# First half prepared by chunk, and the last batch's rows written whole, in a selective-scan and routed-attention kernel

## The chip, the cores and the metric

The kernel runs on one core of a Trainium2 chip, in float32. The metric is the device time of one execution in microseconds (us), a median over runs. On the core, TensorE (PE; PEld is its weight load), VectorE (DVE), ScalarE (ACT) and GpSimd (POOL) compute, each with an instruction queue of its own that it works through in order; SyncE (SP) and the queues of ACT and POOL issue transfers (DMAs), which sixteen DMA engines carry out. SBUF and PSUM are the memories on the core.

## The reference

Inputs are `x`, 16 batches of 1024 tokens and 512 channels, and weights. Two layers follow one another, both with a residual:

```python
# layer 1: selective scan over the tokens, 16 states a channel
xn = layernorm(x)
xp = xn @ x_proj_w.T                  # 64 + 16 + 16 columns: rank, B, C
delta = softplus(xp[..., :64] @ dt_proj_w.T + dt_proj_b)
h = exp(delta * A) * h + delta * B * xn        # A = -exp(A_log), token after token
x1 = x + sum_over_states(h * C) + xn * D

# layer 2: the 127 tokens of a batch with the highest router weight, and no others,
# go through attention and a feed-forward net
y = layernorm(x1)
w = y @ router_w + router_b
sel = the 127 tokens of largest w, in the order of tokens
x2 = block(y[sel])                    # attention with RoPE and mask, GELU net, residuals
out = x1 + where(selected, w * x2, y)
```

(`block`'s RMS norms, mask and heads play no part in the change. One more token, the one at the threshold, counts as not selected.)

## The kernel before

**Layer 1** (`scan_layer`) handles a batch in two halves of 512 tokens; there are 32 halves. A half has 16 states times 4 chunks of 128 channels, 64 steps (`per_half`), one hardware scan (`recur`, L329) of 128 channels by 512 tokens each. The order of all work is written out by hand (`tc.manual_schedule()`): a loop over the steps issues, for each, the diagonal matrices from memory (`diagonals`, L283), scaled rows (`scaled`, L296), decays (`decays`, L304), matmuls that bring the input products into place (`turn`, L316 and L318), the scan, and what follows it. Beside this loop run generators that are advanced once a step; `until(k)` lets one wait for step `k` of the half.

What a half needs beforehand is made by two of these generators, under the half before it. `stats(b)` takes mean and variance of 8 tiles of 128 tokens (`bn_stats` and `bn_aggr`, L138 and L139, on DVE) and makes `rstd` and `off` of them (Ln L142, Exp L144 on ACT, L146 on DVE). `prep(b, half)` normalises 4 tiles (L160, ACT), transposes them (L169, PE; L171, ACT), projects (L176, L180), stores the C rows and the diagonals of B to memory (L183, L187), and computes softplus per chunk of 128 channels (L208 to L218) up to a sum `rest` and an argument `delta`. At step `LN_AT` = 40 one Ln runs over all of `delta` (L230, 128 by 2048), POOL adds `rest` in two instructions (L233), PE transposes the result (L243), and DVE multiplies it with the normalised tokens to `du` (L247).

The first half has no half before it. There, ahead of the loop, the kernel issues `load(0)` (two DMAs of 1 MB, L119, on SP's queue), all of `stats(0)`, `cleared(0)`, a DMA that fills a 2 MB field in memory with zeros (L109, ACT's queue), and all of `prep` for the first half, each drained to its end. `cleared(1)` fills the second field. Only then the loop starts. The zero tile that `cleared` reads shares four buffers with the diagonals `dg`. The constants (`xp_sb` L70, `dt_sb` L74 and L75, `a_sb` L79 with its Exp on ACT L80 and the sign on DVE L81, `d_row` L83, from it `d_ps` L85 and `d_col` L87, `eye` L92, `skip` L95) stand ahead of the hand-written part, and a scheduler places them; they use the same queues.

**Layer 2** (`ffn_layer`) runs the 16 batches as a pipeline of stages (`scores`, `select`, `keep_others` and `attention`, `feed`), 28 steps a period. `select` computes each token's rank and gathers the selected rows of `x1` (`x1_sel`, printed as `x_sel`, L730) and of the mask (L726) with indirect DMAs. `keep_others` writes every row of `out` (L797): `x1 + y` for a token that isn't selected, `x1` for one that is. `feed`, the last stage, adds the net's result to `xs` (L944), multiplies by the router weight (L945), and adds the 127 rows to `out` with an indirect DMA that accumulates in memory (L946, issued by POOL). After the last batch's one the program ends.

Of the kernel before, what the change touches and what calls it, by code (L numbers as in the profile page):

```python
# [10 lines left out]
F32 = mybir.dt.float32  # L11
I32 = mybir.dt.int32
U32 = mybir.dt.uint32
AF = mybir.ActivationFunctionType
ALU = mybir.AluOpType
# [4 lines left out]
P = 128  # L20
# [7 lines left out]
def _drain(gen):  # L28
    for _ in gen:
        pass  # L30
# [3 lines left out]
def scan_layer(ctx, tc, x, x1_dram, a_log, dskip, xpT, dtT, dtb, ident):  # L34
# [9 lines left out]
    nc = tc.nc  # L44
    B, L, D = x.shape
    N = a_log.shape[1]
    R, E = dtT.shape[0], xpT.shape[1]
    ND = D // P
    NT = L // P
    LH = 512  # L50
    NH = L // LH
    TH = LH // P
# [10 lines left out]
    pool = ctx.enter_context(tc.tile_pool(name="s_pool", bufs=2))  # L63
# [2 lines left out]
    psy = ctx.enter_context(tc.tile_pool(name="s_psy", bufs=1, space=PSUM))  # L66
    psm = ctx.enter_context(tc.tile_pool(name="s_psm", bufs=4, space=PSUM))

    xp_sb = const.tile([P, ND, E], F32, tag="xp_sb", name="xp_sb")
    nc.sync.dma_start(xp_sb, xpT.rearrange("(c p) e -> p c e", p=P))  # L70

# [39 lines left out]
            zero.rearrange("p c q -> p (c q)").unsqueeze(1).to_broadcast([P, N, TD * P]),  # L111
        )

    xt, norm, ready, carry, rows_c = {}, {}, {}, {}, {}

    def load(b):
        xt[b] = pool.tile([P, NT, D], F32, tag="xt", bufs=1, name=f"xt_{b}")
        for q in range(NH):
            nc.sync.dma_start(  # L119
                xt[b][:, q * TH : (q + 1) * TH, :],  # L120
                x[b, q * LH : (q + 1) * LH, :].rearrange("(c p) d -> p c d", p=P),
            )

    clock = [0]

    def until(k):
        while clock[0] < k:
            yield

    def stats(b):  # L130

        st = small.tile([P, NT, nc.vector.BN_STATS_DIM], F32, tag="st", name=f"st_{b}")
        mv = small.tile([P, NT, nc.vector.BN_AGGR_DIM], F32, tag="mv", name=f"mv_{b}")
        rstd = small.tile([P, NT], F32, tag="rstd", name=f"rstd_{b}")
        off = small.tile([P, NT], F32, tag="off", name=f"off_{b}")
        for c in range(NT):
            yield from until(25 + 7 * c // 4)
            nc.vector.bn_stats(st[:, c, :], xt[b][:, c, :])  # L138
            nc.vector.bn_aggr(mv[:, c, :], st[:, c, :])  # L139

        yield from until(LN_AT)
        nc.scalar.activation(rstd, mv[:, :, 1], AF.Ln, bias=eps)  # L142
        yield from until(LN_AT + 1)
        nc.scalar.activation(rstd, rstd, AF.Exp, scale=-0.5)  # L144
        yield from until(LN_AT + 3)
        nc.vector.scalar_tensor_tensor(off, mv[:, :, 0], -1.0, rstd, ALU.mult, ALU.mult)  # L146
        norm[b] = (rstd, off)

    def bank(name):
        return psm.tile([P, 512], F32, tag="m", name=name)  # L150
# [1 line left out]
    def prep(b, half):  # L152

        s = f"{b}_{half}"
        rstd, off = norm[b]
        u = pool.tile([P, TH, D], F32, tag="u", bufs=1, name=f"u_{s}")
        for c in range(TH):
            yield from until(1 + c)
            q = half * TH + c
            nc.scalar.activation(  # L160
                u[:, c, :], xt[b][:, q, :], AF.Identity,
                bias=off[:, q : q + 1], scale=rstd[:, q : q + 1],
            )
        uT = pool.tile([P, ND, LH], F32, tag="uT", name=f"uT_{s}")
        for c in range(TH):
            yield from until(10 + 2 * c)
            tp = bank(f"tpu_{s}_{c}").rearrange("p (c f) -> p c f", c=ND)
            for dc in range(ND):
                nc.tensor.transpose(tp[:, dc, :], u[:, c, dc * P : (dc + 1) * P], ident)  # L169
            yield from until(11 + 2 * c)  # L170
            nc.scalar.copy(uT[:, :, c * P : (c + 1) * P], tp)  # L171
        yield from until(19)
        pp = bank(f"pp_{s}")
        for dc in range(ND):
            yield from until(19 + dc // 2)
            nc.tensor.matmul(  # L176
                pp[:E, :], xp_sb[:, dc, :], uT[:, dc, :], start=(dc == 0), stop=(dc == ND - 1)
            )
        yield from until(21)
        nc.scalar.copy(xp[:E, :], pp[:E, :])  # L180
        yield from until(22)
        bc = dram.tile([N, LH], F32, tag="bc", name=f"bc_{s}")
        nc.sync.dma_start(bc, xp[R + N : E, :])  # L183
        h = halves.index((b, half))
        rows_c[h] = bc
        for c in range(TD):
            nc.sync.dma_start(  # L187
                fields[h % 2].rearrange("n (p r) -> n p r", r=TD * P + 1)[:, :, c * P],
                xp[R : R + N, c * P : (c + 1) * P],
            )  # L190
        tb = bank(f"tb_{s}")[:, : TH * 2 * N].rearrange("p (c e) -> p c e", c=TH)
        for c in range(TH):
            nc.tensor.transpose(
                tb[:, c, :], xp[R:E, c * P : (c + 1) * P], ident[R:E, R:E]
            )
        yield from until(23)
        bT = small.tile([P, TH, N], F32, tag="bT", name=f"bT_{s}")
        nc.scalar.copy(bT, tb[:, :, :N])


        delta = pool.tile([P, ND, LH], F32, tag="delta", name=f"delta_{s}")
        rest = pool.tile([P, ND, LH], F32, tag="rest", bufs=1, name=f"rest_{s}")

        def softplus(dc, k):
            yield from until(k)
            z = bank(f"z_{s}_{dc}")
            e, t = delta[:, dc, :], rest[:, dc, :]
            nc.tensor.matmul(z, dt_sb[:, dc * P : (dc + 1) * P], xp, start=True, stop=True)  # L208
            yield from until(k + 1)
            nc.scalar.activation(e, z, AF.Abs)  # L210
            nc.scalar.activation(e, e, AF.Exp, scale=-1.0)
            yield from until(k + 2)
            nc.vector.scalar_tensor_tensor(t, z, 0.0, e, ALU.max, ALU.add)
            yield from until(k + 3)
            w = bank(f"w_{s}_{dc}")
            nc.scalar.add(w, e, 1.0)
            yield from until(k + 4)
            nc.vector.scalar_tensor_tensor(  # L218
                t, w, 1.0, t, ALU.subtract, ALU.subtract, reverse1=True
            )  # L220

        under = [softplus(dc, 24 + 3 * dc) for dc in range(ND)]
        while under:
            for one in list(under):
                if next(one, "end") == "end":
                    under.remove(one)
            if under:
                yield
        yield from until(LN_AT)
        nc.scalar.activation(delta, delta, AF.Ln, bias=1.0)  # L230
        for dc in range(0, ND, 2):
            yield from until(LN_AT + 2 + dc)
            nc.gpsimd.tensor_tensor(  # L233
                delta[:, dc : dc + 2, :], delta[:, dc : dc + 2, :], rest[:, dc : dc + 2, :], ALU.add
            )

        du = pool.tile([P, TH, D], F32, tag="du", name=f"du_{s}")
        ready[b, half] = (uT, delta, du, bT)
        for i, c in enumerate((2, 3, 1, 0)):
            yield from until(49 + 2 * i)  # L240
            tp = bank(f"tpd_{s}_{c}")
            for dc in range(ND):
                nc.tensor.transpose(  # L243
                    tp[:, dc * P : (dc + 1) * P], delta[:, dc, c * P : (c + 1) * P], ident
                )
            yield from until(50 + 2 * i)
            nc.vector.tensor_tensor(du[:, c, :], tp, u[:, c, :], ALU.mult)  # L247
# [133 lines left out]
    dg_of, v_of, da_of, db_of = {}, {}, {}, {}  # L381
    hc_of, ct_of, ct_next, ys_of = {}, {}, {}, {}
    with tc.manual_schedule():
        load(0)
        clock[0] = per_half
        _drain(stats(0))
        cleared(0)
        _drain(prep(*halves[0]))
        cleared(1)
        live[0] = ready.pop(halves[0])  # L390
        for n in range(0, 2 * G, G):
# [49 lines left out]
def ffn_layer(  # L441
# [40 lines left out]
    def load(b, q, tag):  # L482
        if (tag, b, q) in x1_of or not 0 <= b < B:
            return
        x1_of[tag, b, q] = keep.tile([P, 2, D], F32, tag=tag, bufs=3, name=f"{tag}_{b}_{q}")
        nc.sync.dma_start(x1_of[tag, b, q], x1_dram[b][:, q : q + 2, :])
# [175 lines left out]
    def select(b):  # L662
# [116 lines left out]
        nc.vector.tensor_scalar(trig[:, 2, :], trig[:, 1, :], -1.0, None, ALU.mult)  # L779
        yield from until(24)  # L780
        hnT = gained(turned(hn, f"hn_{b}"), 0, f"hnT_{b}", "hnT")
        picked[b] = (xs, sd, at, ms, trig, hnT)

    def keep_others(b):

# [13 lines left out]
            )  # L799

    def attention(b):
        xs, sd, at, ms, trig, hnT = picked.pop(b)
        def projected(name, k):
            ps = psm.tile([P, D], F32, tag="mm", name=f"{name}_ps_{b}")
            for c in range(ND):
# [95 lines left out]
        h2 = rmsnormed(xs, f"h2_{b}")  # L901
        yield from until(23)
        h2T = gained(turned(h2, f"h2_{b}"), 1, f"h2T_{b}", "qT")
        attended[b] = (xs, sd, at, h2T)

    def feed(b):
        xs, sd, at, h2T = attended.pop(b)
        gT = {}

        def unit(f):  # L910
# [24 lines left out]
        for k in sorted(plan):  # L935
# [6 lines left out]
                )  # L942
        yield from until(24)
        nc.vector.tensor_tensor(xs, xs, ff_ps, ALU.add)  # L944
        nc.vector.tensor_scalar(xs, xs, sd[:, WT : WT + 1], None, ALU.mult)  # L945
        nc.gpsimd.indirect_dma_start(  # L946
            out_rows, bass.IndirectOffsetOnAxis(ap=at[:KC, 2:3], axis=0), xs[:KC, :], None,
            compute_op=ALU.add,
        )

    with tc.manual_schedule():
        for p in range(-2, B + 1):
# [82 lines left out]
```

## Time and profile before

| | |
|---|---|
| median of 3 runs | 4037.91 us (4037.52 to 4040.02) |
| the profiled execution | 4038.12 us, its span 4036.3 us |
| mean granted TensorE clock | 0.959 |
| busy, share of the span | PE 89%, DVE 85%, ACT 79%, POOL 67% |
| first scan starts, last scan starts | 50.8 us, 2881.2 us |
| last scatter issued, span ends | 4007.35 us, 4036.3 us |

A line of the timeline has start and duration in us, the engine, the line of the kernel, the operation, output and inputs by the program's names, and in brackets how long the engine had been idle and what released it. "SPq", "ACTq" and "POOLq" are the queues' own instructions, among them the issue of a DMA. The granted clock (PEclk) is the share of full speed that the chip gave to TensorE. Under "DMA share" stands the mean busy share of the sixteen DMA engines, so one engine alone is 0.06. Durations are from the one profiled execution.

### The profile page before, as it was taken

The page shows a single profiled execution, that of the slowest core. Times are in us where ns is not written, and L with a number is a line of the kernel's source. Part 1 is how long each engine was busy: PE and PEld are TensorE (multiplying, and loading weights), DVE is VectorE, ACT ScalarE, POOL GpSimd, SP SyncE. Part 2 cuts the span into 40 slices and gives each one's busy share as a digit, 9 for nine tenths or more (in the row PEclk, how much of TensorE's full clock was granted, in tenths as well). Part 3 has the DMA queues.
Part 4 walks back from the last instruction along what each step waited for, and adds up shares of the span by engine and source line. Part 5 has one row for each costly group of instructions (what it writes and reads, how often), then busy time and mean ns, then how long its engine had stood idle before and what let it go on. Part 6 is the DMA issues. An engine that isn't in the chain of part 4 may idle for free.

```text
span 4036.3 us, 89081 instructions
## 1 busy us (share of the span) xinstructions
PE 3607.3 (89%) x35349; PEld 2272.0 (56%) x35349; DVE 3439.1 (85%) x5142; ACT 3169.2 (79%) x5525; POOL 2716.9 (67%) x1454
## 2 busy tenths in 40 slices
PE   6999999998999999999999999899638999999996
PEld 4666666655666665566666656566324555555453
DVE  5999999999999999999999999999666776867741
ACT  6999999999999999999999999999415455455552
POOL 4899999988999998899999889999600111010110
PEclk8999999999999999999999999999758999999998
DMA  5343433434343343434344343433453434434331
GB/s 152 88 121 82 121 102 103 110 99 122 85 121 95 107 106 106 120 83 121 82 120 111 100 122 86 117 85 104 126 190 106 146 92 154 128 110 150 109 92 33
DMA packets 367466, 444.48 MB, mean 110 GB/s; under 512 B 182381, under 2 KB 252185, under 8 KB 362442
## 3 DMA queue, kind: packets, MB, share of 16 engines
q1 hardware_dynamic: 317080, 371.32, 30.4%
q0 software_dynamic: 40960, 50.55, 6.6%
q10 hardware_dynamic: 9010, 16.91, 1.1%
q8 instruction: 279, 4.57, 0.5%
q14 instruction: 137, 1.12, 0.1%
HBM read 361.36 MB, written 110.66 MB: 117 GB/s over the span
## 4 chain that ended last, share of the span: by engine, by line
PE 44%; DVE 36%; ACT 10%; issue 5%; DMA 3%; POOL 1%; POOLq 0%; DVEq 0%; ACTq 0%; SPq 0%
DVE da L329 19%; PE db L316 13%; PE y L360 8%; PE db L318 6%; PE ff_ps L939 4%; ACT da L304 4%; PE pp L176 3%; ACT v L296 2%; DVE junk L680 2%; DVE junk L676 2%; PE tpy L262 2%; DVE st L630 1%; PE at_ps L896 1%; DVE xw L633 1%; PE tpu L169 1%
## 5 line engine op out<-in xcount | busy, mean ns | idle before, releaser
L341 POOL TENSOR_TENSOR hc<-da,ct 128x1024 f32<-128x1024 f32 x1024 | 2410.5, 2389 | 250.3 <-DVE da L329 193.2
L304 ACT ACTIVATE da<-delta,a_sb 128x512 f32<-128x512 f32 x2048 | 1403.5, 712 | 33.5 <-POOL carry L347 28.5
L316 PE MATMUL db<-dg,du 128*128 128x128 f32 x7168 | 1262.9, 293 | 149.4 <-DVE da L329 130.8
L316 PEld LDWEIGHTS db<-dg,du 128*128 128x128 f32 x7168 | 970.7, 191 | 718.3 <-DVE da L329 542.4
L329 DVE TENSOR_TENSOR_SCAN da<-da,carry,db 128x512 f32<-128x512 f32 x1024 | 1227.7, 1258 | 59.3 <-PE db L318 59.3
L329 DVE TENSOR_TENSOR_SCAN da<-da,db 128x512 f32<-128x512 f32 x1024 | 1175.3, 1197 | 75.1 <-PE db L318 55.3
L318 PE MATMUL db<-ident,v 128*128 128x128 f32 x4608 | 842.1, 274 | 0.0
L296 ACT ACTIVATE v<-du,bT 128x512 f32<-128x512 f32 x1152 | 822.6, 714 | 11.8 <-DVE du L247 6.2
L360 PE MATMUL y<-hc,eye 32*32 32x512 f32 x16384 | 633.0, 606 | 3.2 <-POOL hc L341 2.9
L318 PEld LDWEIGHTS db<-ident,v 128*128 128x128 f32 x4608 | 577.0, 143 | 0.0
L705 POOL PARTITION_ALL_REDUCE thr<-thr_s x16 | 6.2, 385 | 488.0 <-DVE thr_s L704 488.0
L946 POOL DMA_INDIRECT out<-xs,at x16 | 76.0, 4748 | 360.9 <-DVE trig L779 263.0
L939 PE MATMUL ff_ps<-w_sb,gT 128*128 128x512 f32 x512 | 278.3, 663 | 0.0
L914 PE MATMUL up<-w_sb,h2T 128*128 128x512 f32 x512 | 240.5, 598 | 4.0 <-DVE h2T L599 4.0
L360 PEld LDWEIGHTS y<-hc,eye 32*32 32x32 f32 x16384 | 141.0, 103 | 128.9 <-issue 87.2
L208 PE MATMUL z<-xp,dt_sb 97*128 97x512 f32 x256 | 141.6, 636 | 45.1 <-DVE da L329 43.2
L233 POOL TENSOR_TENSOR delta<-delta,rest 128x1024 f32<-128x1024 f32 x64 | 152.0, 2375 | 31.9 <-ACT delta L230 31.9
L593 ACT COPY gT<-tp_g 128x512 f32<-128x512 f32 x64 | 38.2, 596 | 165.6 <-PE tp_g L588 165.6
L914 PEld LDWEIGHTS up<-w_sb,h2T 128*128 128x128 f32 x512 | 92.7, 191 | 100.5 <-issue 92.6
L863 ACT ACTIVATE a<-a,mx 128x127 f32<-128x127 f32 x256 | 98.8, 387 | 54.5 <-DVE mx L861 52.1
L680 DVE TENSOR_SCALAR_CACHE_REDUCE junk<-w_row,side 128x1024 bf16<-128x1024 f32 (+7 forms) x128 | 103.4, 808 | 44.6 <-DMA w_row<-w_dram 44.6
L939 PEld LDWEIGHTS ff_ps<-w_sb,gT 128*128 128x128 f32 x512 | 95.3, 209 | 65.6 <-issue 65.5
(191 smaller groups left out, 3961.2 us busy)
## 6 DMA issues: line engine op xcount, KB each, us to landing
ct<-bc SPq DMA_DIRECT2D x256, 512.0 KB
dg<-field SPq DMA_DIRECT2D x384, 128.0 KB
xt<-in_x SPq DMA_DIRECT2D x32, 1024.0 KB
x<-in_x SPq DMA_DIRECT2D x16, 2048.0 KB
x<-du POOLq DMA_DIRECT2D x32, 1024.0 KB, 8.0
x1a<-x SPq DMA_DIRECT2D x64, 512.0 KB
x1b<-x SPq DMA_DIRECT2D x64, 512.0 KB
out<-x1b SPq DMA_DIRECT2D x64, 512.0 KB
```

The costliest lines, as they stand in the source:

```text
L208: nc.tensor.matmul(z, dt_sb[:, dc * P : (dc + 1) * P], xp, start=True, stop=True)
L233: nc.gpsimd.tensor_tensor(delta[:, dc : dc + 2, :], delta[:, dc : dc + 2, :], rest[:, dc : dc + 2, :], ALU.add)
L296: nc.scalar.activation(v_of[h, n][:, c - m, :], du[:, c, :], AF.Copy, scale=bT[:, c, n : n + 1])
L304: nc.scalar.activation(da_of[h, n][:, dc, :], live[h][1][:, dc, :], AF.Exp, scale=a_sb[:, dc, n : n + 1])
L316: nc.tensor.matmul(out, live[h][2][:, c, ch], dg[:, c, :], start=True, stop=True)
L318: nc.tensor.transpose(out, v[:, c - m, ch], ident)
L329: nc.vector.tensor_tensor_scan(da[:, dc, :], da[:, dc, :], db_of.pop(g), carry[b][:, dc, n : n + 1] if half else 0.0, ALU.mult, ALU.add,)
L341: nc.gpsimd.tensor_tensor(hc, da_of[h, n][:, dc - 1 : dc + 1, :], ct_of[h][:, n % G, :].unsqueeze(1).to_broadcast([P, 2, LH]), ALU.mult,)
L360: nc.tensor.matmul(ys[i][j * S : (j + 1) * S, :], weights(r, j), rows(r, j), start=start, stop=stop, tile_position=(i * S, j * S),)
L680: nc.vector.tensor_scalar(junk[:, lo:], w_row[:, lo:], mine, None, ALU.is_gt, ALU.add, accum_out=cnt[:, 1, c : c + 1],)
L914: nc.tensor.matmul(up, h2T[:, c, :], w1_sb[:, c, f * 512 : (f + 1) * 512], start=(c == 0), stop=(c == ND - 1),)
L939: nc.tensor.matmul(ff_ps, gT[f][:, c, :], w2_sb[:, f * 4 + c, :], start=(f == 0 and c == 0), stop=(f == UP - 1 and c == 3),)
```

## The change

Two parts of the kernel are changed.

At the start of layer 1, `load(0)` is issued ahead of the constants, its first half in four DMAs of 256 KB, the second in one of 1 MB. `cleared(0)` comes ahead of the statistics. `stats` takes a range of tiles: the first four are drained as before, the other four run as a generator beside `prep` of the first half, both now advanced step by step over 64 steps. For the first half only, `prep` runs Ln, the addition (on DVE instead of POOL) and the transposes chunk by chunk of 128 channels, into four PSUM banks at once, and then the four products to `du`. For all other halves the instructions are the same.

At the end of layer 2, `select` hands `x1_sel` on to `feed`. For batches 0 to 14 the scatter accumulates as before. For the last one, DVE computes `xs * weight + x1_sel`, and the scatter writes these rows without accumulating.

```diff
+    xt, norm, ready, carry, rows_c = {}, {}, {}, {}, {}
+
+    def load(b):
+        xt[b] = pool.tile([P, NT, D], F32, tag="xt", bufs=1, name=f"xt_{b}")
+        parts = [1] * TH + [TH] if b == 0 else [TH] * NH
+        q = 0
+        for m in parts:
+            nc.sync.dma_start(
+                xt[b][:, q : q + m, :],
+                x[b, q * P : (q + m) * P, :].rearrange("(c p) d -> p c d", p=P),
+            )
+            q += m
+
+    load(0)
     xp_sb = const.tile([P, ND, E], F32, tag="xp_sb", name="xp_sb")
...
-    def stats(b):
+    def stats(b, part=range(NT)):
+        if part[0] == 0:
+            norm[b] = [
+                small.tile([P, NT], F32, tag=tag, name=f"{tag}_{b}") for tag in ("rstd", "off")
+            ]
+        rstd, off = norm[b]
+        sel = slice(part[0], part[-1] + 1)
...
-        for c in range(NT):
+        for c in part:
             yield from until(25 + 7 * c // 4)
             nc.vector.bn_stats(st[:, c, :], xt[b][:, c, :])
             nc.vector.bn_aggr(mv[:, c, :], st[:, c, :])
         yield from until(LN_AT)
-        nc.scalar.activation(rstd, mv[:, :, 1], AF.Ln, bias=eps)
+        nc.scalar.activation(rstd[:, sel], mv[:, sel, 1], AF.Ln, bias=eps)
...
         yield from until(LN_AT)
+        du = pool.tile([P, TH, D], F32, tag="du", name=f"du_{s}")
+        ready[b, half] = (uT, delta, du, bT)
+        if h == 0:
+            tp = {c: bank(f"tpd_{s}_{c}") for c in (2, 3, 1, 0)}
+            for dc in range(ND):
+                nc.scalar.activation(delta[:, dc, :], delta[:, dc, :], AF.Ln, bias=1.0)
+                nc.vector.tensor_tensor(delta[:, dc, :], delta[:, dc, :], rest[:, dc, :], ALU.add)
+                for c in tp:
+                    nc.tensor.transpose(
+                        tp[c][:, dc * P : (dc + 1) * P], delta[:, dc, c * P : (c + 1) * P], ident
+                    )
+            for c in tp:
+                nc.vector.tensor_tensor(du[:, c, :], tp[c], u[:, c, :], ALU.mult)
+            return
         nc.scalar.activation(delta, delta, AF.Ln, bias=1.0)
...
     with tc.manual_schedule():
-        load(0)
         clock[0] = per_half
-        _drain(stats(0))
         cleared(0)
-        _drain(prep(*halves[0]))
+        _drain(stats(0, range(TH)))
+        both = [prep(*halves[0]), stats(0, range(TH, NT))]
+        for k in range(per_half):
+            clock[0] = k
+            for one in both:
+                next(one, None)
         cleared(1)
...
-        nc.vector.tensor_scalar(xs, xs, sd[:, WT : WT + 1], None, ALU.mult)
-        nc.gpsimd.indirect_dma_start(
-            out_rows, bass.IndirectOffsetOnAxis(ap=at[:KC, 2:3], axis=0), xs[:KC, :], None,
-            compute_op=ALU.add,
-        )
+        to = bass.IndirectOffsetOnAxis(ap=at[:KC, 2:3], axis=0)
+        if b < B - 1:
+            nc.vector.tensor_scalar(xs, xs, sd[:, WT : WT + 1], None, ALU.mult)
+            nc.gpsimd.indirect_dma_start(out_rows, to, xs[:KC, :], None, compute_op=ALU.add)
+        else:
+            nc.vector.scalar_tensor_tensor(
+                xs, xs, sd[:, WT : WT + 1], x1_sel, ALU.mult, ALU.add
+            )
+            nc.gpsimd.indirect_dma_start(out_rows, to, xs[:KC, :], None)
```

More of the change, by code (lines that the diff above doesn't have):

```diff
@@ L112, in cleared @@
         )
[L114 to L121, printed above, removed]
-            )
     clock = [0]
@@ L128, in until @@
             yield
-    def stats(b):
+    def stats(b, part=range(NT)):
[5 more added lines that the diff above has]
+        sel = slice(part[0], part[-1] + 1)
         st = small.tile([P, NT, nc.vector.BN_STATS_DIM], F32, tag="st", name=f"st_{b}")
         mv = small.tile([P, NT, nc.vector.BN_AGGR_DIM], F32, tag="mv", name=f"mv_{b}")
-        rstd = small.tile([P, NT], F32, tag="rstd", name=f"rstd_{b}")
-        off = small.tile([P, NT], F32, tag="off", name=f"off_{b}")
-        for c in range(NT):
+        for c in part:
             yield from until(25 + 7 * c // 4)
@@ L141, in stats @@
         yield from until(LN_AT)
-        nc.scalar.activation(rstd, mv[:, :, 1], AF.Ln, bias=eps)
+        nc.scalar.activation(rstd[:, sel], mv[:, sel, 1], AF.Ln, bias=eps)
         yield from until(LN_AT + 1)
-        nc.scalar.activation(rstd, rstd, AF.Exp, scale=-0.5)
+        nc.scalar.activation(rstd[:, sel], rstd[:, sel], AF.Exp, scale=-0.5)
         yield from until(LN_AT + 3)
-        nc.vector.scalar_tensor_tensor(off, mv[:, :, 0], -1.0, rstd, ALU.mult, ALU.mult)
-        norm[b] = (rstd, off)
+        nc.vector.scalar_tensor_tensor(
+            off[:, sel], mv[:, sel, 0], -1.0, rstd[:, sel], ALU.mult, ALU.mult
+        )
     def bank(name):
@@ L235, in prep @@
             )
-        du = pool.tile([P, TH, D], F32, tag="du", name=f"du_{s}")
-        ready[b, half] = (uT, delta, du, bT)
         for i, c in enumerate((2, 3, 1, 0)):
@@ L781, in select @@
         hnT = gained(turned(hn, f"hn_{b}"), 0, f"hnT_{b}", "hnT")
-        picked[b] = (xs, sd, at, ms, trig, hnT)
+        picked[b] = (x1_sel, xs, sd, at, ms, trig, hnT)
     def keep_others(b):
@@ L801, in attention @@
     def attention(b):
-        xs, sd, at, ms, trig, hnT = picked.pop(b)
+        x1_sel, xs, sd, at, ms, trig, hnT = picked.pop(b)
         def projected(name, k):
@@ L903, in attention @@
         h2T = gained(turned(h2, f"h2_{b}"), 1, f"h2T_{b}", "qT")
-        attended[b] = (xs, sd, at, h2T)
+        attended[b] = (x1_sel, xs, sd, at, h2T)
     def feed(b):
-        xs, sd, at, h2T = attended.pop(b)
+        x1_sel, xs, sd, at, h2T = attended.pop(b)
         gT = {}
@@ L944, in feed @@
         nc.vector.tensor_tensor(xs, xs, ff_ps, ALU.add)
-        nc.vector.tensor_scalar(xs, xs, sd[:, WT : WT + 1], None, ALU.mult)
-        nc.gpsimd.indirect_dma_start(
-            out_rows, bass.IndirectOffsetOnAxis(ap=at[:KC, 2:3], axis=0), xs[:KC, :], None,
-            compute_op=ALU.add,
-        )
+        to = bass.IndirectOffsetOnAxis(ap=at[:KC, 2:3], axis=0)
[3 more added lines that the diff above has]
+        else:
+            nc.vector.scalar_tensor_tensor(
+                xs, xs, sd[:, WT : WT + 1], x1_sel, ALU.mult, ALU.add
+            )
+            nc.gpsimd.indirect_dma_start(out_rows, to, xs[:KC, :], None)
     with tc.manual_schedule():
```

## The prediction

> **What bounds it now.** I read the cores view first (one core, span 4036.3 us, granted clock 0.959), then the timeline of both ends, because the change touches the stretch ahead of the first scan and the last write, and nothing between. The profiled execution took 4038.12 us: its span and 1.8 us around it. The median of the three runs is 4037.91, so a sum made on this execution loses 0.2 us to be compared with it. A change under 0.2% (8.1 us) is what a measurement here can't tell from none.
>
> The timeline of the opening, start and duration in us:
>
> ```profile
> 2.33 0.93 SPq L119 DMA_DIRECT2D xt<-in_x  x2
> ...
> 4.61 0.26 ACT L80 ACTIVATE a_sb<-a_sb 128x64 f32<-128x64 f32 x1 [0.52 <-DMA a_sb<-in_a_log]
> ...
> 8.20 0.69 DVE L138 BATCH_NORM_STATS2 st<-xt 128x6 f32<-128x512 f32 x1 [3.11 <-DMA xt<-in_x]
> ...
> 16.15 0.30 ACT L142 ACTIVATE rstd<-mv,eps 128x8 f32<-128x8 f32 x1 [9.99 <-DVE mv L139]
> ...
> 18.21 2.93 ACT L160 ACTIVATE u<-xt,off,rstd 128x512 f32<-128x512 f32 x4 [0.24 <-DVE off L146]
> ...
> 38.36 1.91 ACT L230 ACTIVATE delta<-delta 128x2048 f32<-128x2048 f32 x1
> 40.35 4.64 POOL L233 TENSOR_TENSOR delta<-delta,rest 128x1024 f32<-128x1024 f32 x2 [31.93 <-ACT delta L230]
> ...
> 48.34 0.69 DVE L247 TENSOR_TENSOR du<-tpd,u 128x512 f32<-128x512 f32 x1 [0.16 <-PE tpd L243]
> ...
> 50.84 10.29 DVE L329 TENSOR_TENSOR_SCAN da<-da,db 128x512 f32<-128x512 f32 x9 [1.81 <-PE db L318]
> ```
>
> To be seen: a serial chain. The first statistic waits for a 1 MB load until 8.20; eight pairs of statistics fill DVE to 16.1; ACT can't normalise (L160) before 18.21; softplus ends in one long Ln (to 40.27), two POOL additions (to 45.0), the transposes and du, and the first scan runs at 50.84. From there the scan's records in the trace show a locked loop: the first scans of the halves start at 50.8, 144.4, 231.5, 322.3, 409.5 us, and from the second on a half takes 90.75 or 87.15 us by turns, through the end. A loop with such a fixed pace passes an earlier start on whole.
>
> The end, from the timeline, the answer on the tile `out`, and the windows view (us; busy of PE, PEld, DVE, ACT, POOL with counts; granted clock, DMA share, GB/s):
>
> ```profile
> 4005.65 0.69 DVE L944 TENSOR_TENSOR xs<-xs,ff_ps 128x512 f32<-128x512 f32 x1 [29.51 <-PE ff_ps L939]
> 4006.37 0.49 DVE L945 TENSOR_SCALAR xs<-xs,sd 128x512 f32<-128x512 f32 x1
> 4007.35 4.70 POOL L946 DMA_INDIRECT out<-xs,at  x1 [25.80 <-DVE xs L945]
> ```
>
> ```profile
> DMA to landing us min/median/max: 27.0/27.3/27.4
> ```
>
> ```profile
> 3953.40:3956.20 2.80, 1.72 (x5) 1.35 (x6) 2.54 (x8) 2.65 (x15) 0.00 (x0) 0.66 1.01 392
> 3965.40:3967.00 1.60, 1.60 (x5) 0.74 (x4) 0.00 (x0) 0.00 (x0) 0.00 (x0) 1.00 0.87 328
> ...
> 4022.00:4034.00 12.00, 0.00 (x0) 0.00 (x0) 0.00 (x0) 0.00 (x0) 0.00 (x0) 0.50 0.07 13
> ```
>
> After 4007.35 there is only the last accumulating scatter: 27 us with every engine idle. In 4022 to 4034 the DMA share is 0.07, about one engine of sixteen, and the DMA view of that window counts 76 packets: 0.158 us a row, so 127 rows take 20.1 us, one behind the other.
>
> **The end, costed.** L945 becomes a scalar_tensor_tensor: 0.49 becomes 0.69 (the row of L213, same shape), 0.2 us lost on the path. The plain scatter reads nothing back. What a plain 2 KB row costs on one DMA engine: the window at 3953 moves 392 GB/s on all sixteen, 24.5 each, 0.084 us a row; the window at 3965, a single 512 KB write to `out` with its start and end, 328 GB/s, 0.100 us. So 127 rows take 10.6 to 12.7 us, and 7.4 to 9.5 us go. I take 9.2, by the busier window, since a queue of 127 rows runs full; less 0.2 that is 9.0. The 4.70 us that POOL takes to issue I leave as they are: a gather of 128 rows takes only about 1 us there (the group of L726), and the difference I put into a rival. The wait for the scatter of batch 14 stays; that one lands at 4004.24 (the chain of waits) and is 3.1 us early.
>
> The Trainium skill's "DMA: Bandwidth & Descriptors", section "Why a DMA increments its semaphore by 16 and not by 1", says that the number of engines divides the slowest dimension, and that 127 partitions get one engine; by that rule a plain scatter of 127 rows stays on one too. The trace agrees for the accumulating one (share 0.07).
>
> **The beginning, costed.** Three pieces.
>
> (a) The loads. SP's first DMA starts at 0.80, where xt's starts at 2.33. First-half data are 1 MB in four pieces, the constants now behind them. Before, 8.20 - 2.33 = 5.87 us passed from issue to use, some 1.0 of it behind the constants; so the fourth piece is usable at 0.80 + 5.87 - 1.0 = 5.7, and the first three sooner. A pair of statistics takes 0.66 + 0.18, so the fourth ends by 6.6 where the eighth ended at 16.1. From there to L160 the steps are unchanged (Ln 0.30, table load 1.28, Exp 0.21, off 0.17 and the gaps: 16.12 to 18.21, 2.1 us): L160 at 8.7, 9.5 us sooner. Half of this is the load, half the four pairs of statistics that no longer stand ahead. I take 8.5, since the clearing of field 0 (2 MB, L109), issued at 16.49 before, now starts beside the loads, and PE may first stand at d_ps, whose d_row comes behind 2 MB of x.
>
> The same page of the Trainium skill, section "Anatomy of one DMA — SWDGE (gpsimd) path", gives 2.0 us + bytes/436 GB/s for a DMA, a rule against small loads: four of 256 KB one after another would be 10.4 us, an estimate by that page, against 4.4 for one of 1 MB, and the sum by it 4022.8. The trace speaks for overlap: xp_sb, a_sb and d_row are issued 0.5 us apart, and all three were in use or landed before 4.7.
>
> (b) The other four pairs of statistics (4 x 0.84 = 3.4 us) go into DVE's softplus stretch, where DVE works 1.4 of each 1.8 us. Two pairs come ahead of the last steps of the third chunk and two around those of the fourth, so the last statistic ends about 21.8 us after L160 starts; before, Ln's table load began 18.9 after it (37.07) and Ln at 20.2.
>
> (c) Ln by chunk: 4 x 0.63 (a 512-wide row: L211's) from 20.0 to 22.5, no longer held by the last DVE step. The additions move to DVE, 4 x 0.69, from 21.8 to 24.5; POOL's 4.64 us go. Transposes follow chunk by chunk; four remain after the last addition (0.8 us at the half clock), and four du of 0.69 end at 27.5 after L160, where the last ended at 30.8 (49.03). So 3.3 us, with the moved statistics already paid in it; without them it would be some 6. The second Ln and Exp of the statistics cost ACT a table load (1.28), but L304's own load at 48.10 then falls away, and the ACT is waiting for du there. cleared(1) is issued some 5 us later against L160; what waits for it is the fourth dg on SP's queue, needed twelve scans (14 us) in, so it is covered; uncovered it would cost those 5 us.
>
> Sum: 8.5 + 3.3 + 9.0 = 20.8. 4038.1 - 20.8 = 4017.3; against the median **4017**.
>
> **Rivals.**
>
> 1. The constants hold the start. The kernel's constants stand outside the hand-written order, so where Exp of a_sb (L80) falls in ACT's queue is decided by a scheduler. It is first there now, at 4.61. With 2 MB of x ahead on SP, a_sb lands near 11 (x until about 9.3 beside the clearing, then 192 KB and 32 KB). If L80 stays first, Ln's table, Ln, Exp's table, Exp and off follow: L160 at 14.9, only 3.3 sooner: 3.3 + 3.3 + 9.0 = 15.6, 4022. For it: program order puts L80 first. Against: at 9.1 to 11 in the DVE timeline, statistics stand ahead of older copies (L87, L92) that were late, so order goes by readiness.
>
> 2. The same on DVE: d_col (L87), which needs d_row from behind the 2 MB, stands ahead of the statistics; L160 stays near 18: 3.3 + 9.0, 4026.
>
> 3. The four small loads don't overlap. A small DMA here takes 3.3 us from issue to use (a_sb, 1.30 to 4.61); four in a row make the fourth usable at 14.0 instead of 5.7, and the time 4025. The page's fit named above points this way. Against: the 0.5 us spacing of the constants.
>
> 4. The plain scatter spreads over sixteen engines and is issued in 1 us, as the gathers of x_sel do, which land in 6.1 us for the same bytes: 21.2 instead of 9.2 saved, 4005. The trace shows only the accumulating form with 127 rows. The Trainium skill, in the section on the semaphore named above, has this as an exception for some direct copies of 127 partitions; nothing before shows it for an indirect one.
>
> 5. The row's 0.158 us isn't the accumulation but the write from this queue: nothing saved there, 4026. Against it: on this same queue the trace's packets of the gathers move 4 KB in 0.159 us, those of the accumulating x<-du 8 KB in 0.629, twice as long a byte.
>
> 6. Slower: PE's clock. It was granted 0.50 from 34 to 53 us while PE was mostly idle, and 1.00 from 54 on. In the loop PE is busy 123 of 130 us at full clock, so at half clock the loop takes about twice as long, 0.5 us lost for each 1 us. If the shorter opening left the clock at 0.50 into the loop, the gain of 20.8 would be used up after 42 us of it, and 60 us of it would give 4047. For it: the half clock lasted 19 us. Against: it was back within 5 us of steady work (49.08 to 54).
>
> **How the numbers follow.** The forecast 45%; rival 1 25%, 2 8%, 3 2%, 4 11%, 5 4%, 6 5%. The range 4007 to 4026 takes in the forecast and rivals 1 to 3, with the bounds of the row price (1.8 us to the slow side, 0.3 to the fast) and half of what (a) and rival 1 differ by, and leaves out 4, 6 and part of 5. The forecast and rivals 1 to 5 each lie over 8.1 us below 4038; the row price unchanged (5) together with 1, 2 or 3 gives 4031 to 4035, within 0.2%, for which I take 5% out of these. Slower by over 0.2% is rival 6, 5%; faster is the rest, 90%.
>
> **What would show it.** Right: first L138 near 3, L160 near 9, the first scan near 39, halves again at 87.15 and 90.75, and the last scatter landing near 18 us after its issue with a DMA share of 0.07. A first scan near 44 is rival 1, near 47 rival 2 or 3 (3 if the first L138 to fourth L138 are 3 us apart); a landing near 6 is rival 4, near 27 rival 5; PEclk 0.5 beyond 60 us is rival 6. A landing of its predecessor later than L945 would make the sum of the end wrong.

## The result, and the profile after

The changed kernel takes **4021.52 us** (median of 5 runs, 4019.32 to 4022.75) where the kernel before takes 4039.18 on the same chip (5 runs, 4037.52 to 4042.88): a ratio of 0.9954, interval 0.9940 to 0.9969, 17.7 us less. The time lies in the predicted range, 4.5 us above the forecast. The range had been drawn to take in rivals 1 to 3, and what happened at the start is close to rival 1. The sum behind the forecast held in only one of its three terms: one was nearly absent, one was exceeded.

The profiled execution took 4022.08 us with a span of 4020.3 (before 4036.3), at a granted clock of 0.963 (before 0.959). Its timeline of the opening, in the columns explained above:

```profile
0.80 2.49 SPq L77 DMA_DIRECT2D xt<-in_x  x5
...
2.84 0.48 ACTq L124 DMA_DIRECT2D field<-zero  x1
...
3.63 0.69 DVE L147 BATCH_NORM_STATS2 st<-xt 128x6 f32<-128x512 f32 x1 [1.13 <-DMA xt<-in_x]
...
7.71 0.37 SPq L94 DMA_DIRECT2D a_sb<-in_a_log  x1
...
8.25 0.69 DVE L147 BATCH_NORM_STATS2 st<-xt 128x6 f32<-128x512 f32 x1 [2.92 <-DMA xt<-in_x]
...
10.23 0.30 ACT L151 ACTIVATE rstd<-mv,eps 128x4 f32<-128x4 f32 x1 [5.60 <-DVE mv L148]
10.55 1.28 ACT L95 ACT_TABLE_LOAD   x1
...
15.85 0.16 DVE L102 COPY d_col<-d_ps 128x4 f32<-128x4 f32 x1 [5.04 <-PE d_ps L100]
16.90 0.26 ACT L95 ACTIVATE a_sb<-a_sb 128x64 f32<-128x64 f32 x1 [5.07 <-DMA a_sb<-in_a_log]
17.06 0.19 ACT L153 ACTIVATE rstd<-rstd 128x4 f32<-128x4 f32 x1
...
17.49 2.93 ACT L170 ACTIVATE u<-xt,off,rstd 128x512 f32<-128x512 f32 x4 [0.24 <-DVE off L155]
...
37.72 2.19 ACT L246 ACTIVATE delta<-delta 128x512 f32<-128x512 f32 x4
...
39.08 2.46 DVE L247 TENSOR_TENSOR delta<-delta,rest 128x512 f32<-128x512 f32 x4
...
42.86 2.48 DVE L253 TENSOR_TENSOR du<-tpd,u 128x512 f32<-128x512 f32 x4 [1.32 <-PE tpd L249]
...
46.52 3.78 DVE L352 TENSOR_TENSOR_SCAN da<-da,db 128x512 f32<-128x512 f32 x3 [1.10 <-PE db L341]
```

The first statistic now runs at 3.63 instead of 8.20, and four suffice. Yet ACT starts to normalise (L170) at 17.49, where before it did at 18.21. Between Ln (L151) and the statistics' Exp (L153) stands an instruction that has nothing to do with them, the Exp of the constant `a_sb` (L95), which waited 5.07 us in front of ACT's queue for its data. On DVE the copy `d_col` (L102) likewise waited 5.04 us, until 15.85, ahead of `off`. From 17.49 on the stages run as forecast, and the first scan starts at 46.52 instead of 50.84.

The windows view of 4 us each (us; busy of PE, PEld, DVE, ACT, POOL with counts; granted clock, DMA share, GB/s) and the waits of SP in the first 40 us (us in total, times, longest) show why `a_sb` was late:

```profile
8.00:12.00 4.00, 0.00 (x0) 0.00 (x0) 2.32 (x8) 1.58 (x2) 0.28 (x1) 1.00 1.07 386
12.00:16.00 4.00, 0.56 (x2) 0.50 (x2) 0.15 (x1) 0.00 (x0) 0.00 (x0) 1.00 1.08 352
```

```profile
SPq L94 <- DMA dt_sb<-in_dtT: 3.7, 1, 3.7
```

The sixteen DMA engines are full from 8 to 16 us, while ACT does almost nothing: `cleared(0)`'s 2 MB, issued at 2.84, share them with x. And SP issued `a_sb` only at 7.71, after 3.7 us of waiting for `dt_sb` to land, whose semaphore it takes over (see the last section).

The end, from the timeline and a windows answer:

```profile
4001.17 0.69 DVE L970 TENSOR_TENSOR xs<-xs,ff_ps 128x512 f32<-128x512 f32 x1 [29.51 <-PE ff_ps L965]
4001.89 0.75 DVE L977 SCALAR_TENSOR_TENSOR xs<-xs,sd,x_sel 128x512 f32<-128x512 f32 x1
4002.94 2.56 POOL L980 DMA_INDIRECT out<-xs,at  x1 [25.87 <-DVE xs L977]
```

```profile
4008.00:4016.00 8.00, 0.00 (x0) 0.00 (x0) 0.00 (x0) 0.00 (x0) 0.00 (x0) 0.50 0.06 23
```

The scatter is still the last thing, alone, on about one engine (share 0.06), but at 23 GB/s instead of 13. From its issue to its last packet 15.6 us pass instead of 27.2.

Where the 16.0 us of span came from, before against after:

| | before | after | difference |
|---|---|---|---|
| normalising starts | 18.21 | 17.49 | -0.7 |
| from there to the first scan | 32.63 | 29.04 | -3.6 |
| first scan to last scan (2881.17 and 2875.10) | 2830.33 | 2828.58 | -1.75 |
| last scan to the net's last sum (L944, L970) | 1124.48 | 1126.07 | +1.6 |
| from there to the end of the span | 30.65 | 19.17 | -11.5 |

The third row lies in the first half, 91.64 us instead of 93.53, and most of it seems not to come from the change: the kernel before ran at half clock from 69.9 to 73.3 us. `acc128` (below), whose layer 1 is the same, didn't, and its first half takes 91.88. From the windows view of the kernel before, then of `acc128`:

```profile
70.00:80.00 10.00, 10.00 (x112) 6.90 (x81) 7.53 (x7) 9.27 (x16) 6.92 (x5) 0.83 0.28 91
```

```profile
70.00:80.00 10.00, 10.00 (x120) 6.86 (x100) 8.33 (x8) 10.00 (x18) 8.61 (x7) 1.00 0.31 105
```

The later halves are 87.14 and 90.78 us by turns, as before. The fourth row is the spread between executions: kernels with the same instructions in layer 2 up to that point gave 1119.4 to 1126.1 there.

### The profile page after: what moved, and what is told of

Its sections match the earlier page's. It is cut to its first block, busy times and chain, and to the rows that moved or that the text cites. A ratio compares the mean times of both kernels' runs of the same rounds, so it can differ in the third digit from the quotient of the medians.

```text
span 4020.3 us, 89089 instructions
## 1 busy us (share of the span) xinstructions
PE 3603.0 (90%) x35349; PEld 2270.0 (56%) x35349; DVE 3441.8 (86%) x5147; ACT 3168.7 (79%) x5529; POOL 2709.6 (67%) x1452
## 4 chain that ended last, share of the span: by engine, by line
PE 44%; DVE 36%; ACT 11%; DMA 4%; issue 4%; POOL 0%; POOLq 0%; DVEq 0%; ACTq 0%; SPq 0%
DVE da L352 19%; PE db L339 12%; PE y L383 8%; PE db L341 6%; PE ff_ps L965 4%; ACT da L327 4%; PE pp L186 3%; ACT v L319 3%; DVE junk L706 2%; DVE junk L702 2%; PE tpy L285 2%; DVE st L656 2%; PE at_ps L922 1%; DVE xw L659 1%; PE tpu L179 1%
```

## The experiments

In each, the label's kernel stands against the kernel before, with the median, ratio and 95% interval; times inside come from the one profiled execution.

### The end: the accumulation or the number of rows?

My theory was that the accumulation makes a row dear; its rival, that 127 rows on one engine do. Three kernels on one chip (before: 4037.02) complete a square of two by two.

`tail_only`: the kernel before with the change's last scatter alone.

> The kernel before, with the plain scatter of the last batch and nothing else of the change. Theory (the two ends add up): first scan at 50.8 us as before, the last scatter lands 15.6 us after its issue as in the changed kernel (27.2 before), 0.3 us lost to the longer DVE step: 11.3 us faster, near 4027. Rival (the start gave more than the trace of the changed kernel shows, through the loop): under 9 us faster.

`acc128`: the kernel before, still accumulating, but with 128 rows (both diffs shortened). The 128th is the token at the threshold, which isn't selected and gets zero added.

```diff
+        wm = (1 - ident[:, KC:P]) * weight        # last batch: 0 for row 127
-            xs * weight  -> out_rows[at[:KC]],  add
+            xs * wm      -> out_rows[at[:P]],   add
```

> The kernel before, accumulating as before, but the last batch's scatter has 128 rows; the row of the token at the threshold gets a weight of 0, so it adds nothing. Theory (the number of rows, 127, puts all of them on one DMA engine): with 128 rows sixteen engines take 8 rows each, 8 x 0.158 = 1.3 us, POOL issues in about 1 us, and the scatter lands 6 us after its issue instead of 27: 21 us faster, near 4018. Rival (accumulating scatters run on one engine for any number of rows): 128 x 0.158 = 20.2 us, landing stays near 27, no change.

`plain128`: the changed kernel with 128 plain rows; for the 128th, `x1_sel` is first completed to what `out` holds for that token (`xs * ident[:, KC:P] + x1_sel`).

```diff
-            xs * weight + x1_sel  -> out_rows[at[:KC]]
+            xs * wm + x1_sel      -> out_rows[at[:P]]
```

> The changed kernel, its last scatter with 128 rows; the row of the token at the threshold is given the sum that it has in the reference (its own residual, no weight). Theory (127 rows stay on one engine, whether accumulating or not): sixteen engines, landing about 6 us after the issue instead of 15.6, so 9 to 10 us faster than the changed kernel, near 4012. Rival (plain scatters run on one engine for any number of rows): no difference from the changed kernel.

Measured: `tail_only` 4022.92, ratio 0.9963 (0.9949 to 0.9977), 14.1 us less, with 9 to 21 in the interval; `acc128` 4011.53, 0.9939 (0.9925 to 0.9952); `plain128` 4005.24, 0.9920 (0.9907 to 0.9934). From the scatter's issue to its last packet:

| | 127 rows | 128 rows |
|---|---|---|
| accumulating | 27.2 us (before) | 4.3 us (`acc128`) |
| plain | 15.2 us (`tail_only`) | 2.4 us (`plain128`) |

The issue from the timeline of `acc128`, then of `plain128`, then the DMA share of `acc128` over 4.3 us from the issue:

```profile
4003.48 1.57 POOL L952 DMA_INDIRECT out<-xs,at  x1 [25.59 <-DVE xs L951]
```

```profile
3997.83 1.02 POOL L986 DMA_INDIRECT out<-xs,at  x1 [25.85 <-DVE xs L985]
```

```profile
4003.50:4007.80 4.30, 0.00 (x0) 0.00 (x0) 0.00 (x0) 0.00 (x0) 1.55 (x1) 0.82 0.45 61
```

One more row takes 22.9 us off the accumulating scatter and 12.8 off the plain one; dropping the accumulation takes 12.0 off 127 rows and 1.9 off 128. So both theories hold, and the larger cause is the one the change left alone: the share is 0.45 over a window in whose first 2.1 us no row moves, against 0.06, so the rows are spread. The section of the Trainium skill's "DMA: Bandwidth & Descriptors" cited in the prediction, "Why a DMA increments its semaphore by 16 and not by 1", gives sixteen engines for 128 partitions and one for 127; for this indirect scatter the square agrees, with and without accumulation, and the exception that the section has for some direct copies of 127 doesn't appear. `acc128` alone, which drops no accumulation and touches nothing at the start, gains 11.4 us more than `tail_only` beside it, 10.9 of which the two scatters explain (15.2 against 4.3). Both kernels with 128 rows gained more than expected, `acc128` 25.5 us for 21 and `plain128` 14 more than the changed kernel for 9 to 10: I had taken the 6 us of the gathers for their landing, and the last packet came after 4.3 and 2.4.

### The middle: softplus by chunk without the rest

`chunk_only`: the kernel before with the `if h == 0:` block of `prep` alone; loads, clearing, all eight statistics and the end stay.

> The kernel before, with the first half's Ln, addition on DVE and transposes by chunk, and nothing else of the change. Theory (the chunks save some 6 us, of which the moved statistics take 2.4 again in the changed kernel): L160 at 18.2 as before, from there to the first scan 26.5 us (32.6 before, 29.0 changed), first scan near 44.7, 6 us faster. Rival (the saving is only what POOL's two additions cost beyond DVE's): 29 us, first scan near 47.2, 3.5 us faster.

Measured: 4035.62, ratio 0.9995 (0.9986 to 1.0004), no measurable difference in the medians. In its trace, normalising starts at 18.22 and the first scan at 47.06, 28.85 us later (before 32.63): the block does save 3.8 us there, but not the 6 that were forecast for it without moved statistics; it is close to the rival's 29 us and 47.2. The timeline says what is last:

```profile
45.02 1.28 ACT L317 ACT_TABLE_LOAD   x1
...
47.06 9.12 DVE L342 TENSOR_TENSOR_SCAN da<-da,db 128x512 f32<-128x512 f32 x8 [1.64 <-ACT da L317]
```

The last `du` is done 27.2 us after the start of normalising (30.8 before, 27.85 in the changed kernel), so the chunks save 3.6 us up to there, and the moved statistics cost 0.65 us, not some 2.7. And without them ACT loads Exp's table at 45.02, in front of the decays, and the first scan waits for these; in the changed kernel the second half's statistics have loaded that table earlier, in a gap. The first half then takes 94.20 us, 0.7 more than before.

### The opening: which wait holds the start?

Theory: `a_sb` and `d_row` come late and stand ahead of the statistics on ACT and DVE; they are late because SP issues them behind x and because the clearing shares the engines. Rival: the loads of x in small pieces are themselves slow. Three kernels, from the changed one, on one chip (before: 4038.45).

```diff
 consts_first:
+    a_sb, d_row: tiles and nc.sync.dma_start      # ahead of load(0)
     load(0)
 clear_late:
-        cleared(0)
         _drain(stats(0, range(TH)))
+        cleared(0)
 both: the two together
```

> The changed kernel, with the loads of a_sb and d_row ahead of those of x on SP. Theory (two causes held the normalisation at 17.5: the Exp of a_sb, in ACT's queue ahead of the statistics' Exp, waiting for a_sb until 16.9; and behind it the clearing of field 0, which slows the loads of x so that the third statistic starts at 8.25): only the first is taken away, the fourth statistic still ends near 10.3, L170 starts near 12.5, the first scan near 41.5: 5 us faster than the changed kernel. Rival (the clearing is what holds all of it): L170 stays after 16, under 1.5 us faster.

> The changed kernel, with the clearing of field 0 issued behind the first four statistics, as it was before the change. Theory: x then has the DMA engines to itself, the fourth statistic ends near 6.6, and a_sb, behind 2.2 MB at about 330 GB/s, lands near 8 to 9, so L170 starts near 9 to 9.5 and the first scan near 38.3: 8 us faster than the changed kernel. Rival (a_sb is late because its issue waits for the landing of earlier loads, not because of the clearing): a_sb still lands after 14, L170 after 14, under 3.5 us faster.

> Both together: a_sb and d_row ahead of x, the clearing behind the first statistics. Theory (the two causes overlap: with the clearing out of the way a_sb is no longer late): L170 near 9.5, the two small loads in front costing some 0.9, first scan near 38.5, no difference from the clearing alone being moved (within 1 us), 8 us faster than the changed kernel. Rival (the two add up): 3 us or more faster than either alone.

| | median | ratio (95%) | normalising | first scan |
|---|---|---|---|---|
| `consts_first` | 4014.98 | 0.9944 (0.9930 to 0.9957) | 12.78 | 44.75 |
| `clear_late` | 4011.88 | 0.9937 (0.9923 to 0.9950) | 10.81 | 39.76 |
| `both` | 4012.74 | 0.9937 (0.9924 to 0.9951) | 11.72 | 41.21 |

Each set against the kernel before on its own chip, the three medians gain 5.8, 8.9 and 8.0 us on the changed kernel (5, 8 and 8 expected). How much of that is the opening a median can't say, since layer 2 alone differed by up to 6.6 us between the profiled executions. So the times inside the opening count here.

`clear_late`, from its timeline:

```profile
3.45 0.69 DVE L147 BATCH_NORM_STATS2 st<-xt 128x6 f32<-128x512 f32 x1 [0.95 <-DMA xt<-in_x]
...
3.89 1.08 SPq L94 DMA_DIRECT2D a_sb<-in_a_log  x1
...
8.22 0.30 ACT L151 ACTIVATE rstd<-mv,eps 128x4 f32<-128x4 f32 x1 [4.10 <-DVE mv L148]
...
10.64 0.26 ACT L95 ACTIVATE a_sb<-a_sb 128x64 f32<-128x64 f32 x1 [0.61 <-DMA a_sb<-in_a_log]
10.81 2.92 ACT L170 ACTIVATE u<-xt,off,rstd 128x512 f32<-128x512 f32 x4
```

Moving the clearing behind the statistics lets SP issue `a_sb` at 3.89 without a wait, has it in use at 10.64, and normalising starts 6.7 us sooner than in the changed kernel; the first scan moves by 6.8. Clearing put first was thus the costliest single step of the opening. `consts_first` takes the constants out of the way instead and starts 4.7 us sooner, as expected (12.5). `both` is no better than `clear_late` (normalising at 11.72, 9.5 expected): with `a_sb` and `d_row` ahead, the first statistic slips from 3.45 to 5.58.

`consts_first` and `both` missed their first scans (41.5 expected for the former). The projection in the timeline of `consts_first`:

```profile
18.00 5.97 PE L186 MATMUL pp<-uT,xp_sb 128*96 128x512 f32 x8 [0.68 <-ACT uT L181]
```

These eight matmuls take 3.67 us in `clear_late`. Here most are 0.85 us apart instead of 0.43, which is TensorE at half its speed, 2.3 us lost (its granted clock is told of in the last section); and the first scan waited 1.74 us for its `db` instead of 1.04, the same effect again.

Three more, on another chip (before: 4038.68), all from `clear_late`. `one_load`: the first half of x in one DMA of 1 MB. `dt_late`: `dt_sb` issued by SP behind `d_row`, so that it too is out of x's way. `best`: `clear_late` with the scatter of `plain128`.

```diff
 one_load:
-        parts = [1] * TH + [TH] if b == 0 else [TH] * NH
+        parts = [TH] * NH
 dt_late:
-    nc.scalar.dma_start(dt_sb...)                 # two, on ACT's queue
+    nc.sync.dma_start(dt_sb...)                   # two, behind d_row
```

> The changed kernel with the clearing behind the first statistics, and the first half of x in one DMA of 1 MB instead of four of 256 KB. Theory (small loads overlap, so the pieces let the first statistics start early): the first statistic starts near 6 instead of 3.5, the fourth ends near 9.3 instead of 8.2; L170 starts near 11.5 instead of 10.8, since a_sb's Exp holds ACT to 10.6 anyway. Rival (four small loads cost as much as they bring): the fourth statistic ends by 8.2 as well.

> The changed kernel with the clearing behind the first statistics, and dt_sb's two loads on SP behind x and the other constants instead of on ACT beside x. Theory (the third tile of x came only at 6.5 because dt_sb's 128 KB shared the DMA engines from 3 to 5.5): the third statistic starts near 5.2, the fourth ends by 6.9, and L170 starts when a_sb is there, 10.3 to 10.8, the first scan within 0.5 us of 39.8. Rival (the tiles of x come at this pace by themselves): the third statistic still starts after 6.2.

> The changed kernel with the clearing of field 0 behind the first statistics and the last scatter of 128 rows. Theory (the two ends are independent): first scan near 39.8 us and 2.4 us from the scatter's issue to its last packet, as in the two kernels alone, so 7 + 13 = 20 us faster than the changed kernel, a span near 3997 to 4000. Rival (part of the gain of each is run to run variation of the second layer): under 15 us faster.

`one_load`: 4016.63, ratio 0.9947 (0.9931 to 0.9964). From its timeline:

```profile
6.63 0.69 DVE L147 BATCH_NORM_STATS2 st<-xt 128x6 f32<-128x512 f32 x1 [4.13 <-DMA xt<-in_x]
...
11.95 0.18 DVE L148 BATCH_NORM_AGGREGATE mv<-st 128x2 f32<-128x6 f32 x1
...
14.37 2.93 ACT L170 ACTIVATE u<-xt,off,rstd 128x512 f32<-128x512 f32 x4 [0.24 <-DVE off L155]
```

The first statistic comes 3.2 us later than with four pieces, and normalising 3.6, of which 2.2 are the last aggregation's wait behind the copy `eye` (from 9.7 to 11.95), which waited for POOL. So the small pieces overlap and pay, by an estimated 1.4 us at normalising without that wait, and the rival falls. In `clear_late` the four statistics start at 3.45, 4.28, 6.48 and 7.31, and the fourth piece is in use 6.5 us after the first issue (0.80). The estimate in the prediction by the Trainium skill's "DMA: Bandwidth & Descriptors" ("Anatomy of one DMA — SWDGE (gpsimd) path") was 10.4 us for four loads one after another. The trace doesn't agree with one after another for loads issued half a microsecond apart; and the page gives its figure for DMAs that GpSimd issues, while SP issues these, so the estimate used it outside its case.

`dt_late`: 4012.19, ratio 0.9938 (0.9922 to 0.9955). The third statistic starts at 5.71 instead of 6.48, so `dt_sb` was part of its delay; but `a_sb` is in use only at 11.57, and normalising at 11.73, 0.9 later than in `clear_late`. The first scan, at 43.12 (within 0.5 of 39.8 expected), met the slow projection, 5.40 us. Nothing was gained.

`best`: **3998.53 us, ratio 0.9901 (0.9884 to 0.9917)**, 40.1 us below the kernel before and the fastest of all. Its opening is `clear_late`'s, but its projection was slow too (first line, from its timeline), so its first scan starts at 43.13:

```profile
16.21 6.13 PE L186 MATMUL pp<-uT,xp_sb 128*96 128x512 f32 x8 [0.68 <-ACT uT L181]
...
43.13 12.50 DVE L352 TENSOR_TENSOR_SCAN da<-da,db 128x512 f32<-128x512 f32 x11 [1.75 <-PE db L341]
```

## Why the prediction was right, and where it was wrong

**(a) the opening, 8.5 us taken, 0.7 measured: the step that failed.** Two sentences in it were wrong. "The fourth piece is usable at 0.80 + 5.87 - 1.0 = 5.7", with the fourth statistic ending by 6.6: it ended at 10.2, 3.6 us later, since the third tile was waited for until 8.25. The clearing beside the loads was named there and priced, with another doubt, at one microsecond; `clear_late` shows that the fourth then ends at 8.2, so it cost 2.0, and `dt_late` (7.4) that `dt_sb` cost 0.8 more; the last 0.8 stays open. "From there to L160 the steps are unchanged", 2.1 us: it took 7.3, because `a_sb` and `d_col` stood between. 3.6 and 5.2 are the 8.8 us that separate 8.7 from 17.49.

**The mechanism was in rivals 1 and 2, given a third of the chance together.** Rival 1 had it right that a scheduler places the Exp of `a_sb` and that it can hold the statistics' Exp; but it had it ahead of Ln, and in the trace it stands behind. It had `a_sb` landing near 11 and normalising at 14.9, by the bytes ahead of `a_sb` alone. Measured were 16.90 and 17.49. In `clear_late`, `a_sb` is in use at 10.64: of the 6.3 us between, 3.8 lie in front of its issue (7.71 against 3.89), the wait that I hadn't counted, and 2.4 behind it, beside the clearing. `d_col` waited until 15.85, which is rival 2; the copy, `off` behind it and 0.2 us to ACT would have had normalising start near 16.2, so `a_sb` came last. The time, 4021.5, is nearly rival 1's 4022 by two misses that cancel: its first scan came 2.5 us later than the "near 44" it named, and the end gave 2.5 more than its 9.0.

**(b) and (c), 3.3 us taken, 3.6 measured: right in total, with one part mis-sized.** Against the start of normalising, the last statistic ended at 21.7 (21.8 predicted), Ln began at 20.2 (20.0), the additions ran from 21.6 to 24.0 (21.8 to 24.5), the last `du` ended at 27.85 (27.5). Of the 3.6, 0.7 is the wait of the first scan on `db`, 1.10 instead of 1.81, with the clock back sooner; so 2.9 without that. That "without them it would be some 6" was wrong: in `chunk_only` the additions start only 0.7 us sooner against normalising (20.9 against 21.6), which gives 3.6 at the last `du` and, since a table load then becomes last, 3.8 at the first scan. It didn't follow from the prediction's own rows either: Ln by chunk to 22.5, one addition, the last transpose and four `du` end at 26.2, which is 4.6. The moved statistics cost 0.65 at `du` and bring that table load forward. `cleared(1)`, later against normalising, cost nothing that shows: the first half takes 91.64 us, and 91.88 in `acc128` with the old opening.

**The end, 9.0 us taken, 11.5 measured: the mechanism right, one term too small.** The stream of packets, from first to last, took 12.4 us instead of 21.9, 9.5 saved for 9.2 predicted. The multiplication with addition cost 0.26 for 0.2. But I had left POOL's 4.70 us of issue as they were: it took 2.56, and the first packet followed the issue by 3.20 instead of 5.27 us, 2.1 more. In the trace the tiny packets of 8 bytes, which begin ahead of the first row and run beside the first rows, went from 1905 to 945. One engine carried it all, so rival 4 fell for 127 rows, and rival 5 with the halved stream.

**Rivals 3 and 6** didn't happen: `one_load` showed the overlap, and from the second half on the loop kept its two lengths, with no half clock of the opening beyond 49.5 us. That an earlier first scan passes whole through the loop held, with a first half that moved by up to 3 us beside it: measured at the start of the second half, the two executions differ by 6.2 us (144.37 to 138.17), where the first scan says 4.3. Against `acc128` (143.02) it is 4.9, so most of the rest seems to be the stretch at half clock named above: 3.4 us of it go with 1.6 us of time, about the 0.5 for each that rival 6 was priced with.

## What to carry to other kernels

When a load is moved ahead, follow every transfer that now stands behind it to the first instruction that uses it, on that engine's in-order queue: a constant nobody needs yet can hold the statistics that everybody waits for. Look also at what its issue waits for; here it was an unrelated load. A large transfer without urgency, such as a clearing, belongs behind the loads of the critical path, even on another queue, since the DMA engines are shared. And before making a row of a scatter cheaper, look at how many engines carry it: here one padding row was worth more than dropping the accumulation.

## What the runs showed of the hardware that was not expected

- **TensorE's speed just after the opening differs between executions.** The projection of eight matmuls took 3.67 us in the changed kernel, `clear_late`, `both` and `one_load`, but 5.40, 5.97 and 6.13 in `dt_late`, `consts_first` and `best`, though `best` has the instructions of `clear_late` there. The windows view reads a granted clock of 1.00 over these stretches, but only because the trace has no record of the clock there: the first begins at 20.44, 22.65 and 21.20 us in these three, inside the projection, and the matmuls are 0.85 us apart up to it and 0.43 behind it. In `clear_late` it begins at 15.60, ahead of the projection at 16.01. With the wait of the first scan on `db` (1.04 or 1.75) it explains the span from normalising to the first scan: 28.95 in `clear_late`, plus 2.46 and 0.71, is 32.12, and `best` has 32.13. What decides which of the two an execution gets stays open.
- **What the first scan loses to the late clock seems to come back in the first half.** Kernels whose first scan waited 1.74 or 1.75 us had first halves of 90.97 to 91.01 us, those with 1.04 to 1.18 had 91.56 to 91.70. The granted clock goes the same way: its half speed ends 1.2 to 2.0 us after the first scan's start in the former, 2.9 to 3.2 in the latter. That the one causes the other wasn't tried. (This holds for kernels with the changed opening; with the old one the first scan waited 1.64 to 1.81, and the first half took 91.88 to 94.20.)
- **An issue can wait for the landing of an older DMA.** SP held `a_sb` back 3.7 us for `dt_sb`, which it doesn't depend on, and `xp_sb` 0.3 us for `xt`. The program itself asks for these waits: in the trace each DMA names the semaphore that its landing raises, the opening's loads use eight of them in turn, and a DMA that takes one again waits first for the landing of its last user. In the changed kernel `xp_sb`, the ninth, takes that of the first piece of x, and `a_sb`, the tenth, that of `dt_sb`'s first load. In `clear_late`, with the clearing later, `a_sb` is the ninth and takes that of the first piece of x, which was in use at 3.45; it is issued at 3.89 without a wait.
- **Plain rows were merged, accumulating ones weren't.** The 127 plain rows left as 63 packets of 4096 bytes and one of 2048, at about 0.159 us each; the accumulating rows stayed at 2048 bytes. A plain row thus takes 0.08 us on one engine. An accumulating packet lasts 0.178 us in the kernel before and in `acc128` alike; on the one engine of the kernel before, one starts every 0.158.
